# Two moves in a hand-ordered graph kernel: where one unit's selection matrices are made, and where a pair's overflow is taken

## The chip, the cores and the metric

The kernel runs on one core of a Trainium2 chip. A core has five engines that run side by side, each with its own queue of instructions: TensorE (PE, matrix products), VectorE (DVE), ScalarE (ACT), GpSimd (POOL) and SyncE (SP, which issues DMAs). [...] The metric is the device time of one execution in microseconds (us).

## The reference

One layer of message passing on a graph of 6250 nodes and 200000 edges, 128 features:

```python
h = jnp.maximum(_layernorm(x), 0.0)
xw = h @ W_in                                                  # one row per node
W_ij = (softplus(f_ij @ W_f1 + b_f1) - LOG2) @ W_f2 + b_f2     # one row per edge
x_ij = xw[dst] * (W_ij * edge_weight1)
out = jax.ops.segment_sum(x_ij, src, num_segments=6250)        # edges summed by src
y = x + (softplus(out @ W_o1 + b_o1) - LOG2) @ W_o2 + b_o2
```

`dst` is sorted, `src` is not: the sum over `src` is what the kernel spends most of its order on.

## The kernel before

The edges are taken in 391 quads of 512. A quad goes through a pipeline of some five stages, written as one Python loop over items `i`, fully unrolled: item `i` runs the first stage of quad `i`, the second of quad `i - 1`, and so on. Each engine gets its instructions in exactly the order in which the loop writes them; nothing reorders them, and the framework only adds the semaphores and, where a buffer is used again, the wait for its last reader.

Inside an item there are named points, in this order: `L`, `D0`, (`s1_oh`), `D1`, (`s2_pe_x`, `s2_pe_w`, `s1_pe`: matmuls L494, L497, L505, L313), (`s1_exp`, `s1_ln`: L318, L323), `A0`, `A1`, (`s2_copy`: four copies L510 into `xc`), `DM`, (`s2_m`: product L520 of `W` and `xc`), `PE1`, `PE2`, `A2`, `D2`, (scatters), `S`. `at(i, point, fn, ...)` hangs a step on a point of an item; steps on the same point run in the order in which they were hung there.

Edges are summed by `src` in two ways.

- *Plain and listed quads* (223 of 391) are written to DRAM by scatters that add: four DMAs with an index per row for each quad, issued by POOL (`scatter`, L582), whose source tile `s` has four buffers.
- *Grouped quads* (168 of them, `mpq`) are added on the chip. Their distances are 2, 2, 2 and 3 items, so the order repeats every 9 items. Call an item's place its distance from the first grouped quad of its round of four: grouped quads stand at places 0, 2, 4 and 6, and place 0 follows place 8. For a grouped quad `q`, item `q + 1` writes its product into a tile `pt` (L520) and makes four permutation matrices `pm` on DVE (`perm_oh`, L662); item `q + 2` splits the product into three bf16 parts (`part_rem`, two L676 on DVE, and the small `part_ext`, L682 on ACT); from item `q + 3` on PE permutes the edges into slots (`permute`, four times four matmuls L687) and ACT copies the result (`perm_out`, L693, into `mst`). `pm` and `pt` have two buffers each.

Slots can overflow. For each pair of grouped quads (the two at places 0 and 2, or at 4 and 6) `over_pe` collects the overflow rows of both quads in one product (eight matmuls L700 into `po`), and `over_out` copies it out on ACT (L707). Five items later the overflow is summed and scattered too (`over_idx` L714, `over_dg`, `over_row`, `over_eq`, `over_sum` L738 to L740, `over_copy` L745, `over_ji` L750, `over_int` L754).

Every 8 grouped quads (two rounds of four, 18 items) there are four *units*. A unit, at place 2 or at place 6 of a round (`UOFF = (2, 6)`), multiplies the permuted tiles of 8 quads with 8 selection matrices (`unit_pe`, 96 small matmuls L780 into four PSUM buffers `un`) and DVE adds the result to the sum on the chip in the item behind (`unit_evac`, four L791). The selection matrices `so` are made on DVE by `unit_oh` (one L765 each), in two halves of four.

PSUM tiles with the tag "B" share four buffers: `pq`, `po`, `un`, `orow`, `osum`, and the tiles of some rarer steps, among them the preparation of node rows (`prep_tp` L218, `prep_mm` L231) and the counting for the lists (`l_count` L378). A unit needs all four at once.

```python
def over_pe(q):
    qs = mpq[mpi[q] // 2 * 2:mpi[q] + 1]
    t = ps.tile([P, 512], F32, tag="B", name="po", bufs=4)
    for c in range(4):
        for h, p in enumerate(qs):
            nc.tensor.matmul(t[h * OVC:(h + 1) * OVC, :PW], mp[p]["pm"][:, c, GRP * CAP:],
                             high(mp[p]["pt"][:, c:c + 1, :PW])[:, 0], start=(c == 0), stop=(c == 3))
    mp[q]["po"] = t, len(qs) * OVC
```

After the loop a short tail adds the four DRAM sums and runs the last two layers.

Of the kernel before, what the change touches and what calls it, by code (L numbers as in the profile page):

```python
# [27 lines left out]
MP0 = 8  # L28
MPGAPS = (2, 2, 2, 3)
# [4 lines left out]
UOFF = (2, 6)  # L34
# [20 lines left out]
def tile_gnn(ctx: ExitStack, tc: tile.TileContext, x, fB, cT, srcT, srcr, dstr, win_, wf1, wf2, bias, bo1c, wo1,  # L55
# [25 lines left out]
    mpq = sorted_quads(NQ)  # L81
    mpi = {q: n for n, q in enumerate(mpq)}
# [752 lines left out]
    with tc.manual_schedule():  # L835
# [112 lines left out]
        def at(i, point, fn, *a):  # L948
            hooks.setdefault((i, point), []).append((fn, a))
# [136 lines left out]
        if spread:  # L1086
            k = clear(mid + 9, busy, 2)
# [3 lines left out]
            k = clear(NQ - 1, busy, 2)  # L1091
# [21 lines left out]
        for r in range(-(-len(mpq) // RKQ)):  # L1113
            i = mpq[RKQ * r]
            at(i - 5, "D2", rank_group, r)
            k = clear(i - 4, units)
            at(k, "PE2", rank_count, r)
            at(k + 1, "D0", rank_own, r)
            k = clear(k + 1, units)
# [5 lines left out]
        for w in range((LE - LB) // SW):  # L1125
# [25 lines left out]
            k = clear(i + 1, units)  # L1151
# [10 lines left out]
        for q in mpq:  # L1162
            at(q + 1, "D2", perm_oh, q)
            at(q + 2, "D2", part_rem, q, 1)
            at(q + 2, "D2", part_rem, q, 2)
            at(q + 2, "A2", part_ext, q)
            if q + 4 in units:
                for s in range(4):
                    at(q + 3, "PE2", permute, q, s)
                for s in range(4):  # L1170
                    at(q + 3, "PE2", perm_out, q, s)
            else:
                for s in range(4):
                    at(q + 3 + s // 2, "PE2", permute, q, s)
                    at(q + 4 + s // 2, "A0", perm_out, q, s)
            if mpi[q] % 2 or q == mpq[-1]:
                at(q + 3, "PE1", over_pe, q)
                at(q + 3, "PE1", over_out, q)
                at(q + 5, "DM", over_idx, q)
                at(q + 6, "A0", over_dg, q)  # L1180
                k = clear(q + 6, units)
                at(k, "PE2", over_row, q)
                at(k + 1, "D0", over_eq, q)
                k = clear(q + 8, units)
                at(k, "PE2", over_sum, q)
                at(k + 1, "A0", over_copy, q)
                at(k + 1, "DM", over_ji, q)
                at(k + 1, "A2", over_int, q)
                at(k + 2, "S", over_scatter, q)
        last = mpq[-1]  # L1190
        for r in range(len(mpq) // RND):
            for s, k in enumerate(unit_slots(mpq, r)):
                at(k - 2, "D2", unit_oh, r, s, 0)
                at(k - 1, "D2", unit_oh, r, s, 1)
                at(k, "PE2", unit_pe, r, s)
                at(k + 1, "D1", unit_evac, r, s)
# [79 lines left out]
    with tc.For_i(0, trips, 1) as ci:  # L1276
# [55 lines left out]
        s = wk.tile([P, P], F32, bufs=1, tag="dg", name="fs")  # L1332
# [112 lines left out]
def sorted_quads(nq):  # L1445
    qs, q = [], MP0
    while q < nq - MPEND:
        qs.append(q)
        q += MPGAPS[(len(qs) - 1) % len(MPGAPS)]
    return qs if len(qs) % RND <= EXTRA else qs[:len(qs) // RND * RND]  # L1450
# [7 lines left out]
def unit_slots(qs, r):  # L1458
    if r == len(qs) // RND - 1:
        return [qs[-1] + 6 + 2 * s for s in range(4)]  # L1460
    per, end = sum(MPGAPS), qs[RND * r + RND - 1] + 5
    return [i for i in range(end, end + 4 * per) if (i - MP0) % per in UOFF][:4]
# [12 lines left out]
def clear(i, busy, n=1):  # L1475
    while any(i + k in busy for k in range(n)):
        i += 1
    return i
# [113 lines left out]
```

## Time and profile before

| what | value |
|---|---|
| timed runs (3) | 2068.21, 2069.33, 2073.08 us; median 2069.33 us |
| the profiled execution | 2067.92 us, its span 2066.1 us |
| mean granted TensorE clock | 0.961 |
| busy: PE, DVE, ACT, POOL | 1815.0, 1658.7, 1468.1, 1648.0 us |
| scatters on POOL (L582): listed, plain, overflow | 768, 123, 96 |

All rows of the profile are of that one execution. "Busy" is the time in which an engine executes something; waiting and issuing do not count. A line `L582` is a line of the kernel's file. In the timelines a row gives the start and the length in us, the engine, the line, the operation, what it writes and reads, how many instructions the row joins, and in brackets how long the engine had been idle and what ended that. Matmuls are pipelined and their ends are modelled, so neighbouring rows of PE can overlap a little.

### The profile page before, as it was taken

To read this page: it belongs to the slowest core of one execution; us is meant where nothing else is said; L and a number is where in the kernel's file an instruction comes from. 1 tells how busy PE (TensorE), PEld (TensorE's weight loads), DVE (VectorE), ACT (ScalarE), POOL (GpSimd) and SP (SyncE) were. 2 spreads that over 40 slices of the span, in tenths; PEclk is the share of its full clock that TensorE was granted. 3 is DMA by queue.
4 is the path that set the end of the run, shared out by engine and by line. 5 is a ranking of instruction groups with operands and counts; after the bars stand their busy time and mean duration, and the time that the engine had idled before them with its cause. 6 is when DMAs were issued, how large, how long until landed. Compare 5 with 4: busy or idle time off the path is not lost. (4 is left out here: it accounts for less than half of the span.)

```text
span 2066.1 us, 54971 instructions
## 1 busy us (share of the span) xinstructions
PE 1815.0 (88%) x19121; PEld 1190.5 (58%) x19121; DVE 1658.7 (80%) x4448; ACT 1468.1 (71%) x3999; POOL 1648.0 (80%) x1040
## 2 busy tenths in 40 slices
PE   3589899989988999999899899899998999999956
PEld 2455556556655666555566566565665666566734
DVE  3678788888987888888888888879889788787745
ACT  3368676877776788777778777777777777788714
POOL 3578888888888788887788888888888888888774
PEclk9679999999999999999999999999999999999978
DMA  6887666667666666666667676676766666666649
GB/s 242 226 212 153 120 119 118 130 110 136 126 124 116 117 139 123 125 123 122 118 123 132 118 131 116 115 132 107 136 120 119 117 119 118 101 121 131 131 46 243
DMA packets 381177, 272.39 MB, mean 132 GB/s; under 512 B 97727, under 2 KB 341354, under 8 KB 380898
## 3 DMA queue, kind: packets, MB, share of 16 engines
q0 software_dynamic: 143728, 71.30, 34.6%
q1 hardware_dynamic: 236882, 197.50, 33.0%
q8 instruction: 151, 2.47, 0.5%
q14 instruction: 128, 1.05, 0.2%
q10 hardware_dynamic: 288, 0.07, 0.0%
HBM read 154.45 MB, written 114.24 MB: 130 GB/s over the span
## 5 line engine op out<-in xcount | busy, mean ns | idle before, releaser
L582 POOL DMA_INDIRECT acc<-s,lji x768 | 1254.4, 1633 | 255.9 <-issue 191.3
L687 PE MATMUL pq<-pt,pm 128*128 128x387 bf16 x2688 | 535.7, 343 | 29.8 <-ACT pt L682 13.5
L510 ACT ACTIVATE xc<-xg,cb 128x128 f32<-128x128 f32 x1564 | 448.2, 377 | 89.9 <-PE xg L497 85.3
L505 PE MATMUL W<-w,a 128*128 128x128 f32 x3128 | 465.1, 293 | 0.0
L505 PEld LDWEIGHTS W<-w,a 128*128 128x128 f32 x3128 | 389.5, 196 | 42.2 <-issue 3.1
L780 PE MATMUL un<-so,mst 32*128 32x392 bf16 x8064 | 376.6, 329 | 19.8 <-DVE lbad L411 4.6
L687 PEld LDWEIGHTS <-pm 128*128 128x128 bf16 x2688 | 259.7, 100 | 217.0 <-issue 40.8
L693 ACT CAST mst<-pq 128x387 bf16<-128x387 f32 x672 | 302.3, 481 | 112.8 <-PE pq L687 110.8
L780 PEld LDWEIGHTS <-mst 32*128 32x128 bf16 x8064 | 230.9, 94 | 158.7 <-issue 59.2
L323 ACT ACTIVATE a<-a,con 128x512 f32<-128x512 f32 x391 | 282.3, 722 | 12.7
L582 POOL DMA_INDIRECT acc<-s,ji x123 | 197.4, 1605 | 78.3 <-issue 28.3
L318 ACT ACTIVATE a<-z 128x512 f32<-128x512 f32 x391 | 238.5, 610 | 24.6 <-PE z L313 14.5
L676 DVE TENSOR_TENSOR pt<-pt 128x512 f32<-128x512 f32 x336 | 231.7, 690 | 5.8
L662 DVE TENSOR_SCALAR pm<-iot,pos 128x576 bf16<-128x576 f16 x672 | 220.8, 390 | 0.0
L520 DVE TENSOR_TENSOR s<-W,xc 128x512 f32<-128x512 f32 x192 | 131.9, 687 | 81.0 <-ACT xc L510 61.1
L765 DVE TENSOR_SCALAR so<-iot,mst 128x392 bf16<-128x392 f16 x672 | 191.9, 345 | 5.7 <-PE un L780 5.6
L791 DVE TENSOR_TENSOR accT<-un,accT 128x392 f32<-128x392 f32 x320 | 158.5, 557 | 44.7 <-PE un L780 44.2
L582 POOL DMA_INDIRECT acc<-os,oji x96 | 154.6, 1610 | 29.4 <-issue 19.5
L497 PE MATMUL xg<-wn,oh 63*128 63x128 bf16 x1564 | 157.4, 222 | 17.5 <-ACT xc L510 10.0
L520 DVE TENSOR_TENSOR pt<-W,xc 128x512 f32<-128x512 f32 x168 | 115.4, 687 | 70.4 <-ACT xc L510 58.6
L313 PE MATMUL z<-ft,ws 123*128 123x512 bf16 x391 | 151.7, 388 | 15.3 <-DMA ft<-fsd 15.0
L494 PE MATMUL W<-b2rep,onesb 64*128 64x512 bf16 x391 | 154.0, 394 | 0.0
(209 smaller groups left out, 1975.7 us busy)
## 6 DMA issues: line engine op xcount, KB each, us to landing
rb<-reld SPq DMA_DIRECT2D x391, 64.0 KB
fsd<-f SPq DMA_DIRECT2D x49, 480.0 KB
ft<-fsd SPq DMA_DIRECT2D x195, 120.0 KB
sb<-src SPq DMA_DIRECT2D x169, 128.0 KB
fb<-in_fB_dram SPq DMA_DIRECT2D x49, 320.0 KB
ft<-fsd SPq DMA_DIRECT2D x195, 80.0 KB
wn<-tab SPq DMA_DIRECT2D x782, 15.8 KB
acc<-s,lji POOLq DMA_INDIRECT x768
```

Source lines behind the costliest of these rows:

```text
L318: nc.scalar.activation(a, st[q]["z"], AF.Exp)
L323: nc.scalar.activation(a, a, AF.Ln, bias=half, scale=0.5)
L505: nc.tensor.matmul(W[:, c, :], st[q]["a"][:, c * P:(c + 1) * P], w2, start=False, stop=(c == 3))
L510: nc.scalar.mul(xc[:, c, :], st[q]["xg"][:, c, :], late["c", q // CQ][:, 4 * (q % CQ) + c:4 * (q % CQ) + c + 1])
L520: nc.vector.tensor_tensor(m[:, :, :P], st[q]["W"], st[q]["xc"], op=ALU.mult)
L582: nc.gpsimd.indirect_dma_start(out=accs[k][:rows, :], out_offset=bass.IndirectOffsetOnAxis(ap=ji, axis=0), in_=s, in_offset=None, compute_ ...
L662: nc.vector.tensor_scalar(pm[:, c], iot[:, :SLOTS], rk[r]["pos"][:, 4 * j + c:4 * j + c + 1], None, op0=ALU.is_equal)
L676: nc.vector.tensor_tensor(pt[:, :, k * P:(k + 1) * P], a, high(a), op=ALU.subtract)
L687: nc.tensor.matmul(t[:, :PW], mp[q]["pm"][:, c, s * P:(s + 1) * P], high(mp[q]["pt"][:, c:c + 1, :PW])[:, 0], start=(c == 0), stop=(c == 3))
L693: nc.scalar.copy(mp[q]["ms", s][:, :PW], mp[q].pop(("q", s))[:, :PW])
L765: nc.vector.tensor_scalar(so, iotw[:, :GN], w[:, 3 * P // 2:3 * P // 2 + 1], None, op0=ALU.is_equal)
L780: nc.tensor.matmul(ts[g][:, :GN], mp[q]["ms", s][v, k * P:(k + 1) * P], mp[q]["oh"][v], start=(q == qs[0] and k == 0), stop=(q == qs[-1] a ...
```

## The change

Two points of the order move; no instruction is added, removed or altered.

- `over_pe` and `over_out` of a pair are hung on the item behind the next grouped quad instead of on item `q + 3` (`q` is the pair's second quad). For a pair whose second quad stands at place 2 that is the same item, place 5. For one whose second quad stands at place 6 it is one item later: place 1 instead of place 0.
- For a unit at place 6 (all but the very last units) the first half of the selection matrices is made in item `k - 1` instead of `k - 2`, so both halves, eight L765, stand one behind the other at place 5. Units at place 2 keep their halves in two items.

```diff
             if mpi[q] % 2 or q == mpq[-1]:
-                at(q + 3, "PE1", over_pe, q)
-                at(q + 3, "PE1", over_out, q)
+                k = mpq[mpi[q] + 1] + 1 if mpi[q] + 1 < len(mpq) else q + 3
+                at(k, "PE1", over_pe, q)
+                at(k, "PE1", over_out, q)
                 at(q + 5, "DM", over_idx, q)
...
             for s, k in enumerate(unit_slots(mpq, r)):
-                at(k - 2, "D2", unit_oh, r, s, 0)
+                at(k - (1 if (k - MP0) % sum(MPGAPS) == UOFF[1] and k < last else 2), "D2", unit_oh, r, s, 0)
                 at(k - 1, "D2", unit_oh, r, s, 1)
                 at(k, "PE2", unit_pe, r, s)
```

In the order of each engine this shows as follows. On PE the eight L700 of place 0 stand behind L313 of place 1, ahead of `over_sum`. On ACT L707 stands behind the four L510 of place 1 instead of those of place 0. On DVE four L765 leave their place behind L676 at place 4 and stand ahead of the other four behind L662 at place 5; L520 at place 1 gets a wait for L700 in place of one for L505. POOL and SP keep their order.

## The prediction

> **What bounds the kernel now.** I read the page first, then the busy time by stretches, then what POOL waited for, and last the timelines of PE, DVE and ACT around the items that the diff touches. The page's first part names PE as the busiest engine:
>
> ```profile
> PE 1815.0 (88%) x19121; PEld 1190.5 (58%) x19121; DVE 1658.7 (80%) x4448; ACT 1468.1 (71%) x3999; POOL 1648.0 (80%) x1040
> ```
>
> PE has 88%, POOL 80%. That order misleads, because a scatter on POOL (L582) is never followed by the next one at once. What POOL waited for between 364 and 1210 us (columns: engine and line, releaser, us in total, times, longest):
>
> ```profile
> POOL acc L582 <- issue: 106.1, 348, 0.3
> POOL acc L582 <- DVE s L520: 15.1, 12, 2.9
> POOL acc L582 <- DVE bn L186: 8.1, 6, 3.7
> ```
>
> The first row is a fixed pause: 106.1 / 348 = 0.305 us before a scatter, with nothing to wait for. Only the other two rows are waits for data, and both are the product of item `q` (`s2_m`, L520) coming too late. So a scatter holds POOL for its own time and 0.305 us. With that price the busy time by stretches (each row: the stretch, its length, then busy us and count of PE, PEld, DVE, ACT, POOL) reads differently:
>
> ```profile
> 364.00:660.00 296.00, 270.23 (x2908) 174.27 (x2907) 251.18 (x699) 223.35 (x616) 249.62 (x153) 0.98 0.68 123
> 660.00:1210.00 550.00, 506.82 (x5523) 329.89 (x5520) 474.56 (x1317) 412.55 (x1134) 448.29 (x276) 0.98 0.67 124
> 1210.00:1765.00 555.00, 515.46 (x5677) 333.53 (x5674) 468.84 (x1230) 418.36 (x1130) 467.76 (x287) 0.99 0.66 120
> 1765.00:1900.00 135.00, 130.20 (x1354) 87.22 (x1353) 107.18 (x270) 112.07 (x311) 113.34 (x72) 0.98 0.67 116
> 1900.00:2007.00 107.00, 88.85 (x1038) 62.58 (x1035) 67.38 (x176) 54.38 (x159) 86.04 (x56) 0.93 0.58 97
> ```
>
> POOL's time with the pauses: 249.62 + 153 x 0.305 = 296.3 of 296; 448.29 + 276 x 0.305 = 532.5 of 550; 467.76 + 287 x 0.305 = 555.3 of 555; 113.34 + 72 x 0.305 = 135.3 of 135; 86.04 + 56 x 0.305 = 103.1 of 107. In three of the five stretches the scatters stand end to end, and what PE, DVE and ACT save there shortens nothing: it only lengthens the queue in front of POOL. POOL ran dry for 17.5 us between 660 and 1210 and for 3.9 us at the end. The granted clock is 0.98 in the first of these, so the clock is no term here. Ahead of 364 us I count nothing, because the start-up sets the scatters there.
>
> So the change can bring at most 17.5 + 3.9 = 21.4 us, and it brings what it takes off the chain of PE, DVE and ACT from about 364 to 1210 us (before that POOL's queue is full; from there to 660 it drains, so a lead won there is kept) and in the last 240 us.
>
> **Part 1: the overflow product.** Places count the items from a round of four grouped quads, 0 to 8. `over_pe` (eight matmuls, L700) and its copy `over_out` (L707) move from place 0 to place 1, for one pair in two; the pair at place 5 stays, and so does every other instruction of the pair. Work is neither added nor removed, so the question is what waits. PE at a place 0 (start, us, engine, line, what; in brackets the idle time and who ended it):
>
> ```profile
> 951.95 0.38 PE L313 MATMUL z<-ft,ws 123*128 123x512 bf16 x1
> 952.26 0.36 PE L700 MATMUL po<-pt,pm 128*64 128x387 bf16 x1
> 953.69 0.86 PE L700 MATMUL po<-pt,pm 128*64 128x387 bf16 x7 [1.07 <-DVE pt L676]
> 954.48 0.71 PE L231 MATMUL xps<-win_sb,h 128*128 128x128 f32 x4
> 955.03 0.54 PE L378 MATMUL lcnt<-wgtb,eql 128*128 128x1 bf16 x16
> 955.43 0.86 PE L687 MATMUL pq<-pt,pm 128*128 128x387 bf16 x4
> ```
>
> The first of the eight runs, the other seven wait for the remainders (`part_rem`, L676) of the pair's second quad. The permutations behind them (L687) read the same remainders, so the wait does not vanish: it passes to L687. What changes is that the work between them, which does not need the remainders (L231 and L378, 955.43 - 954.48 = 0.95 us), now runs inside the wait. L313 ends at 952.33, L231 and L378 at 953.28, and L687 starts at 953.69 instead of 955.43. Of those 1.74 us, 0.79 (953.69 to 954.48) are `over_pe` and come back in the next item; 0.95 us are won. Where a place 0 has no wait, or nothing between, nothing is won.
>
> Between 364 and 1210 us there are 19 places 0. Seven have both a wait and work between. The first and the last of them, by the same reading (the pair's matmuls are over where L231 starts):
>
> ```profile
> 414.22 0.71 PE L231 MATMUL xps<-win_sb,h 128*128 128x128 f32 x4
> 414.76 0.54 PE L378 MATMUL lcnt<-wgtb,eql 128*128 128x1 bf16 x16
> 415.17 0.33 PE L687 MATMUL pq<-pt,pm 128*128 128x387 bf16 x1
> ```
>
> ```profile
> 1130.00 0.49 PE L231 MATMUL xps<-win_sb,h 128*128 128x128 f32 x2
> 1130.33 0.54 PE L378 MATMUL lcnt<-wgtb,eql 128*128 128x1 bf16 x16
> 1130.73 0.33 PE L687 MATMUL pq<-pt,pm 128*128 128x387 bf16 x1
> ```
>
> That is 0.95 and 0.73 us. The seven, each the smaller of wait and work, are 0.95, 0.48, 0.48, 0.83, 0.15, 0.95 and 0.73: 4.6 us. The last 240 us hold three more places 0; the estimate for them is one such gain, 0.9 us (bounds 0 and the 3.9 us that POOL was dry).
>
> The move puts a new wait on DVE and puts `over_out` behind `xc` on ACT. ACT, DVE and PE at places 1 and 2 of the same round:
>
> ```profile
> 957.40 1.15 ACT L510 ACTIVATE xc<-xg,cb 128x128 f32<-128x128 f32 x4
> 958.41 0.43 ACT L248 CAST x<-rm 128x256 bf16<-128x256 f32 x1
> 958.71 0.64 ACT L318 ACTIVATE a<-z 128x512 f32<-128x512 f32 x1
> 959.37 0.72 ACT L323 ACTIVATE a<-a,con 128x512 f32<-128x512 f32 x1
> 960.00 0.25 ACT L745 COPY os<-osum 128x132 f32<-128x132 f32 x1
> 960.15 0.87 ACT L693 CAST mst<-pq 128x387 bf16<-128x387 f32 x2
> ```
>
> ```profile
> 958.58 0.69 DVE L520 TENSOR_TENSOR pt<-W,xc 128x512 f32<-128x512 f32 x1 [1.54 <-ACT xc L510]
> ```
>
> ```profile
> 961.45 0.38 PE L313 MATMUL z<-ft,ws 123*128 123x512 bf16 x1
> 961.76 0.35 PE L780 MATMUL un<-so,mst 32*128 32x392 bf16 x4
> ```
>
> DVE: `part` has two buffers, so the grouped product at place 1 (the L520 above) overwrites the tile that `over_pe` still reads, and must wait until `over_pe` is through. Behind it on DVE stand `perm_oh` (L662), four selection matrices (L765) and the next `oh`. Today it waits anyway, 1.54 us for `xc`. After the change item 1 begins 1.74 us earlier, `xc` with it, and `over_pe` is done about 0.9 us before 958.58 (1.74 less its own 0.79). So the new wait takes the place of the old one and ends earlier. That lead on DVE pays only where DVE, not PE, is the last to arrive at the unit's evacuation: bounds 0 and 2.4 us over the 19 rounds, and I take 1, nearer to 0, since the evacuation mostly waits for the unit itself.
>
> ACT: the unit at place 2 (L780) needs all four PSUM buffers, and the last to be freed is the second L693, at 961.02, 0.74 us before 961.76. `over_out` is a copy of the same shape as one of the two L693 (0.87 / 2 = 0.44 us) and now stands between L510 and L248. With `over_pe` done at about 957.7, `over_out` ends at about 958.2 and the five behind it, 2.61 us from 958.41 to 961.02, at 960.8; the unit, 0.95 earlier, wants to start at 960.8. The slack is used up to nothing. Bounds: 0, and the whole 0.44 at each of 19 + 5 units; I take 0.5 us in all, nearest to the row.
>
> **Part 2: the selection matrices at place 6.** Four L765 leave place 4 and stand in front of the other four at place 5, behind L520 and `perm_oh`. Nothing else moves with them. DVE at places 4 to 6 of another round:
>
> ```profile
> 1021.99 1.41 DVE L676 TENSOR_TENSOR pt<-pt 128x512 f32<-128x512 f32 x2
> 1023.32 1.05 DVE L765 TENSOR_SCALAR so<-iot,mst 128x392 bf16<-128x392 f16 x4
> 1024.29 0.68 DVE L520 TENSOR_TENSOR pt<-W,xc 128x512 f32<-128x512 f32 x1
> 1024.89 0.81 DVE L284 TENSOR_TENSOR f<-fr,f 128x640 bf16<-128x640 f32 x1
> 1025.62 1.25 DVE L662 TENSOR_SCALAR pm<-iot,pos 128x576 bf16<-128x576 f16 x4
> 1026.79 1.27 DVE L765 TENSOR_SCALAR so<-iot,mst 128x392 bf16<-128x392 f16 x4
> ```
>
> ```profile
> 1029.39 0.34 PE L780 MATMUL un<-so,mst 32*128 32x392 bf16 x3
> ```
>
> ```profile
> 1029.78 0.22 DVE L750 SCALAR_TENSOR_TENSOR ojd<-os,con,ojd 128x1 f32<-128x1 f32 x1 [1.31 <-ACT os L745]
> 1030.82 0.69 DVE L520 TENSOR_TENSOR s<-W,xc 128x512 f32<-128x512 f32 x1 [0.82 <-ACT xc L510]
> ```
>
> The remainders are made before the four L765, so `over_pe` at place 5 is not helped. L520 waits for `over_pe` and would not start earlier than 1024.29 here; DVE would stand idle for the 1 us that the four now fill, and everything behind would come 1.05 us later: L765 ends at 1029.1 instead of 1028.0. The unit starts at 1029.39 and takes its matrices one after the other, and L750 waited 1.31 us for ACT: 1.05 fits under both. If that cover is gone (rounds where DVE is late at place 6), the cost is bounded by the same 1.05 us; but in those rounds DVE reaches L520 after `over_pe` is done, so nothing idles and the order alone changes. I take 0 for all, bounds -1 and +3 us.
>
> A scatter beside such a run, from the same stretch:
>
> ```profile
> 1026.24 1.54 POOL L582 DMA_INDIRECT acc<-s,lji  x1 [0.31 <-issue]
> ```
>
> It ran with `perm_oh` and L765 all along and took 1.54 us, less than the mean (448.29 / 276 = 1.62). [...]
>
> **The sum.** 4.6 + 0.9 + 1.0 - 0.5 + 0 = 6.0 us less. The profiled execution took 2067.92 us (span 2066.1), below the three timed runs (median 2069.33); it would take 2061.9, and the median 2063.3. A measurement of this kernel can tell about 0.3% (6.2 us) from no change, so the forecast lies right beside that bound.
>
> **Rivals.** *Wider gain* (12%): the lead on DVE and the freer ACT at place 0 also carry through places 3 to 8, and POOL hardly runs dry: 12 to 20 us, about 2054. For it: both L520 rows wait for ACT. Against: the remainders that PE waits for at place 5 do not move. *No gain* (11%): the filler at place 0 waits for its own inputs, or the lead is lost at the next wait for L676: 2069. *ACT holds the unit at place 2* (15%, slower): the second L693 ends later than the unit could start. The place is the unit behind `over_out`; there are 24 of them in the two stretches that count. From 5.5 / 24 = 0.23 us late each it eats the gain, from (5.5 + 6.2) / 24 = 0.49 it makes the kernel slower by over 0.3%; at 0.7 (`over_out` and its wait for `over_pe`) it costs 24 x 0.7 - 5.5 = 11 us: 2080. For it: the slack of 0.74 is the only one. Against: item 1 starts earlier on ACT by the wait that `over_out` leaves behind at place 0. [...]
>
> **How the numbers follow.** The forecast has 60%; its own range is 2059 to 2068 (4.6 less some 3 us for ACT or for Part 2 leaves 1.6; 4.6 with 1.9 at the end, 2.4 on DVE and 1 from Part 2 makes 10), and 26 of the 60 lie below 2063.1. Faster: 26 + 12 = 38%. Same: 34 + 11 = 45%. Slower: 15 + 2 = 17%. The range, 2053 to 2074, leaves out a third of the wider gain and most of the slower cases.
>
> **What would show it.** Right: at place 0 the wait for L676 stands before L687, with L231 and L378 ahead of it; L520 at place 1 waits for `over_pe`; POOL's wait for L520 between 660 and 1210 falls from 23 us to about 18 while its busy time stays. Wrong: L780 at place 2 waits for ACT's L693; scatters longer than before; POOL's waits for L520 as large as now or in new stretches.

## The result, and the profile after

| | before | with the change |
|---|---|---|
| median of 9 runs | 2069.33 us (2064.84 to 2075.11) | 2056.89 us (2052.48 to 2061.75) |
| the profiled execution | 2067.92 us, span 2066.1 | 2059.12 us, span 2057.4 |

The ratio is 0.9934 with a 95% interval of 0.9916 to 0.9953: the change makes the kernel faster by 0.66%, by the medians 12.4 us. The prediction's sum was 6.0 us less, 2063.3 us. The direction was right and the size about half of what came. The two profiled executions show 8.8 us of it.

The first part of the page, with the change:

```profile
PE 1808.0 (88%) x19121; PEld 1183.3 (58%) x19121; DVE 1657.7 (81%) x4448; ACT 1472.2 (72%) x3999; POOL 1642.0 (80%) x1040
```

What POOL waited for between 364 and 1210 us, and its busy time in the stretch in which it ran dry (POOL's pair of numbers is the fifth):

```profile
POOL acc L582 <- issue: 102.8, 337, 0.3
...
POOL acc L582 <- DVE s L520: 6.9, 7, 2.5
POOL acc L582 <- DVE bn L186: 6.4, 3, 3.2
```

```profile
660.00:1210.00 550.00, 509.24 (x5547) 329.96 (x5547) 476.58 (x1322) 417.14 (x1144) 454.64 (x278) 0.98 0.68 124
```

The waits for `s` fell from 15.1 + 8.1 to 6.9 + 6.4 us, and with the pause POOL's time is 454.64 + 278 x 0.305 = 539.4 of 550 instead of 532.5: 10.6 us dry instead of 17.5. That is 6.9 us of the 8.8.

PE at the same place 0 as in the prediction, and the two items behind it:

```profile
945.07 0.38 PE L313 MATMUL z<-ft,ws 123*128 123x512 bf16 x1
945.29 0.61 PE L231 MATMUL xps<-win_sb,h 128*128 128x128 f32 x4
945.73 0.54 PE L378 MATMUL lcnt<-wgtb,eql 128*128 128x1 bf16 x16
946.81 1.57 PE L687 MATMUL pq<-pt,pm 128*128 128x387 bf16 x8 [0.54 <-DVE pt L676]
...
949.95 0.89 PE L700 MATMUL po<-pt,pm 128*64 128x387 bf16 x8
...
954.08 3.16 PE L780 MATMUL un<-so,mst 32*128 32x392 bf16 x72
```

L231 and L378 stand inside the wait, of which 0.54 us is left. L700 runs an item later without a wait, and from L313 to the unit it takes 954.08 - 945.07 = 9.01 us instead of 961.76 - 951.95 = 9.81. DVE and ACT at place 1:

```profile
950.94 0.69 DVE L520 TENSOR_TENSOR pt<-W,xc 128x512 f32<-128x512 f32 x1 [1.67 <-PE po L700]
```

```profile
950.91 0.48 ACT L707 CAST mo<-po 128x387 bf16<-128x387 f32 x1 [0.96 <-PE po L700]
...
953.00 0.87 ACT L693 CAST mst<-pq 128x387 bf16<-128x387 f32 x2
```

L520 waits for `over_pe` now, but starts 950.94 - 945.07 = 5.87 us after L313 where it took 6.63. The second L693 ends at 953.87, 0.21 us ahead of the unit: the slack of 0.74 us shrank and held.

The place 6 of the prediction's second set of rows (DVE, then the unit on PE):

```profile
1014.23 1.41 DVE L676 TENSOR_TENSOR pt<-pt 128x512 f32<-128x512 f32 x2
1016.77 0.69 DVE L520 TENSOR_TENSOR pt<-W,xc 128x512 f32<-128x512 f32 x1 [1.14 <-PE po L700]
...
1019.23 2.43 DVE L765 TENSOR_SCALAR so<-iot,mst 128x392 bf16<-128x392 f16 x8
...
1023.37 0.22 DVE L750 SCALAR_TENSOR_TENSOR ojd<-os,con,ojd 128x1 f32<-128x1 f32 x1 [1.31 <-ACT os L745]
```

```profile
1022.98 1.25 PE L780 MATMUL un<-so,mst 32*128 32x392 bf16 x19
```

Where four L765 stood before L520, DVE idles 1.14 us; the eight end at 1021.66, the unit starts at 1022.98, and L750 waits for ACT by the same 1.31 us as before.

### The profile page after: what moved, and what is told of

Same layout as the page of the kernel before. It is cut to its first block, busy times and chain, and to the rows that moved or that the text cites. A ratio compares the mean times of both kernels' runs of the same rounds, so it can differ in the third digit from the quotient of the medians.

```text
span 2057.4 us, 54972 instructions
## 1 busy us (share of the span) xinstructions
PE 1808.0 (88%) x19121; PEld 1183.3 (58%) x19121; DVE 1657.7 (81%) x4448; ACT 1472.2 (72%) x3999; POOL 1642.0 (80%) x1040
## 5 line engine op out<-in xcount | busy, mean ns | idle before, releaser
L510 ACT ACTIVATE xc<-xg,cb 128x128 f32<-128x128 f32 x1564 | 449.5, 378 | 86.2 <-PE xg L497 83.7
L505 PE MATMUL W<-w,a 128*128 128x128 f32 x3128 | 465.6, 293 | 0.0
L505 PEld LDWEIGHTS W<-w,a 128*128 128x128 f32 x3128 | 389.9, 196 | 42.3 <-issue 3.3
L780 PE MATMUL un<-so,mst 32*128 32x392 bf16 x8064 | 371.0, 325 | 18.9 <-ACT s L540 4.5
L693 ACT CAST mst<-pq 128x387 bf16<-128x387 f32 x672 | 303.5, 482 | 115.6 <-PE pq L687 112.7
L780 PEld LDWEIGHTS <-mst 32*128 32x128 bf16 x8064 | 225.0, 93 | 158.1 <-issue 52.6
L676 DVE TENSOR_TENSOR pt<-pt 128x512 f32<-128x512 f32 x336 | 231.9, 690 | 5.8
L662 DVE TENSOR_SCALAR pm<-iot,pos 128x576 bf16<-128x576 f16 x672 | 222.0, 392 | 0.0
L520 DVE TENSOR_TENSOR s<-W,xc 128x512 f32<-128x512 f32 x192 | 132.0, 687 | 84.1 <-ACT xc L510 71.4
L765 DVE TENSOR_SCALAR so<-iot,mst 128x392 bf16<-128x392 f16 x672 | 183.5, 337 | 8.0 <-PE un L780 7.9
L520 DVE TENSOR_TENSOR pt<-W,xc 128x512 f32<-128x512 f32 x168 | 115.6, 688 | 88.5 <-PE po L700 52.9
L313 PE MATMUL z<-ft,ws 123*128 123x512 bf16 x391 | 152.2, 390 | 16.0 <-DVE iotl L940 9.3
L494 PE MATMUL W<-b2rep,onesb 64*128 64x512 bf16 x391 | 154.5, 395 | 0.0
```

Of the source, the lines that this page charges most:

```text
L505: nc.tensor.matmul(W[:, c, :], st[q]["a"][:, c * P:(c + 1) * P], w2, start=False, stop=(c == 3))
L510: nc.scalar.mul(xc[:, c, :], st[q]["xg"][:, c, :], late["c", q // CQ][:, 4 * (q % CQ) + c:4 * (q % CQ) + c + 1])
L520: nc.vector.tensor_tensor(m[:, :, :P], st[q]["W"], st[q]["xc"], op=ALU.mult)
L662: nc.vector.tensor_scalar(pm[:, c], iot[:, :SLOTS], rk[r]["pos"][:, 4 * j + c:4 * j + c + 1], None, op0=ALU.is_equal)
L676: nc.vector.tensor_tensor(pt[:, :, k * P:(k + 1) * P], a, high(a), op=ALU.subtract)
L693: nc.scalar.copy(mp[q]["ms", s][:, :PW], mp[q].pop(("q", s))[:, :PW])
```

## The experiments

All of them ran against the kernel before on the same chip. The chips differ (the kernel before had medians from 2069.3 to 2078.1 us), so ratios are compared. The code excerpts show the lines that matter.

| kernel | median us | ratio | 95% interval |
|---|---|---|---|
| the change | 2056.89 | 0.9934 | 0.9916 to 0.9953 |
| before, again | 2071.87 | 1.0008 | 0.9989 to 1.0027 |
| Part 1 alone | 2057.06 | 0.9937 | 0.9916 to 0.9958 |
| Part 2 alone | 2071.39 | 1.0004 | 0.9990 to 1.0018 |
| product behind the filler | 2071.22 | 1.0000 | 0.9983 to 1.0018 |
| copy an item later | 2072.96 | 0.9989 | 0.9973 to 1.0004 |
| both of these | 2069.29 | 0.9961 | 0.9940 to 0.9982 |
| change in items 50 to 229 only | 2066.67 | 0.9959 | 0.9941 to 0.9978 |
| change in items 230 to 349 only | 2077.20 | 0.9996 | 0.9979 to 1.0012 |
| before, tiles read earlier | 2070.05 | 0.9959 | 0.9939 to 0.9980 |
| change, tiles read earlier | 2062.32 | 0.9913 | 0.9885 to 0.9942 |
| change, remainders first | 2064.54 | 0.9928 | 0.9902 to 0.9954 |
| change, both of these | 2064.95 | 0.9931 | 0.9907 to 0.9956 |

A second table is worked out from the traces. For the 18 rounds between 364 and 1210 us it sums the length of the items (from the first L494 of one to that of the next) by their place, and beside that stand POOL's waits for L520 and L186 in that stretch, in us:

| kernel | places 0, 1 | place 2 | places 3 to 8 | POOL's waits |
|---|---|---|---|---|
| before | 153.6 | 114.9 | 534.2 | 23.2 |
| before, again | 153.7 | 113.0 | 536.4 | 25.9 |
| Part 2 alone | 152.3 | 114.8 | 535.3 | 21.0 |
| the change | 149.1 | 109.7 | 533.2 | 13.3 |
| Part 1 alone | 148.3 | 109.5 | 532.0 | 16.5 |
| product behind the filler | 150.6 | 119.8 | 533.8 | 24.8 |
| copy an item later | 154.5 | 115.4 | 535.5 | 25.1 |
| both of these | 149.7 | 118.0 | 531.8 | 15.7 |
| before, tiles read earlier | 153.2 | 106.0 | 540.5 | 17.8 |
| change, tiles read earlier | 149.3 | 104.4 | 542.1 | 16.3 |
| change, remainders first | 147.3 | 111.4 | 537.2 | 4.7 |
| change, both of these | 148.0 | 106.7 | 537.3 | 2.3 |
| change in items 50 to 229 only | 150.2 | 111.9 | 536.1 | 19.5 |
| change in items 230 to 349 only | 152.1 | 113.0 | 540.6 | 28.2 |

The last two rows serve as a further trace of each side, since these 18 rounds are items 62 to 223: the first has the change in all of them, the second in none. Each row is one execution, and the rows of one side differ by up to 2.4 us at place 2 and by 6 to 7 us in POOL's waits.

**The kernel before, again.**

> The kernel before, once more, unchanged: it gives a second profile and says how far two executions of one kernel lie apart. Time 2069 +- 3 us. If the difference of 12.4 us between the medians, of which the two profiled executions show 8.8, is in the waits of POOL, then between 364 and 1210 us POOL's waits for L520 and for L186 sum to 21 to 25 us again (23.2 in the first profile, 13.3 with the change), and the scatter before which 300 others stand starts at 661 +- 2 us. If the rest of the difference is scatter time that varies from execution to execution, the sum of the scatters' own time differs by 3 to 6 us from 1606.4.

Its waits were 25.9 us, a little above the range, the scatter before which 300 others stand started at 665.8 us, 3 us outside its range, and POOL was busy for 1643.9 us where the first profile has 1648.0. The change and Part 1 alone have 1642.0 and 1641.3. So 8.5 us of the gain stand in POOL's waits (23.4, the mean of the first three rows, against 14.9, the mean of the next two), and some 4 us in the scatters' own time. With two profiles on the one side that last part is not shown; the change in the middle items alone has 1648.3.

**Part 1 alone, Part 2 alone.** The two hunks of the diff, one at a time.

> Part 1 alone: the overflow product and its copy one item later, the selection matrices as before. Theory A (the filler at place 0 runs inside the wait for L676, Part 2 is worth nothing): 2055 to 2060 us, all of the gain, POOL's waits for L520 and L186 between 364 and 1210 us at 12 to 15 us. Rival B (both parts share the gain, since eight L765 in a row leave DVE free for the remainders at place 4): 2062 to 2064 us. Rival C (Part 2 is the whole gain): 2069 us.

> Part 2 alone: the first half of the selection matrices at place 5, the overflow product as before. Theory A: 2069 +- 3 us; L520 at place 5 waits for L700 in most rounds (12 us in all between 364 and 1210 us instead of 3.6) and nothing behind it is later, as L791 at place 6 waits 2 us in all as before. Rival B: 2062 to 2064. Rival C: 2057. A cost that Part 1 covers would show as 2072 to 2078.

Part 1 is the whole gain, Part 2 is worth nothing that can be measured: theory A had the shares right, and rivals B and C fall. POOL's waits, 16.5 us, lie a little above the 12 to 15 expected. What inside Part 1 pays is the question of the next three runs. What DVE waited for in Part 2 alone, and in the kernel before:

```profile
DVE pt L520 <- PE po L700: 11.7, 10, 2.0
```

```profile
DVE pt L520 <- PE po L700: 3.6, 4, 1.0
```

The idle 8 us on DVE are there, and no cost of them can be seen: the ratio is 1.0004.

**The product behind the filler.**

```diff
-    at(q + 3, "PE1", over_pe, q); at(q + 3, "PE1", over_out, q)
+    at(q + 3, "PE2", over_pe, q); at(q + 3, "PE2", over_out, q)   # second pair only, ahead of permute
```

> The kernel before, with one step moved inside place 0: the overflow product of the second pair stands behind the preparation and counting matmuls (L231, L378) and still ahead of the permutations (L687); it stays in its item, and so does its copy. Theory A (what is won is that this filler runs inside the wait for L676): the same gain as Part 1 at the seven places 0 of the prediction, and no new wait at place 1: 2055 to 2062 us. Rival D (the gain comes from the copy and the product leaving place 0, that is from ACT and DVE at place 0): no gain, 2067 to 2071 us.

This missed: no gain. PE did win at place 0 (153.2, the mean of the first three rows, to 150.6), and place 2 took it all back (114.2 to 119.8). ACT at place 0 of the round shown, before:

```profile
954.59 0.48 ACT L707 CAST mo<-po 128x387 bf16<-128x387 f32 x1 [2.31 <-PE po L700]
```

ACT, then the unit at place 2, with the product behind the filler:

```profile
954.04 0.48 ACT L707 CAST mo<-po 128x387 bf16<-128x387 f32 x1 [2.29 <-PE po L700]
...
959.46 0.87 ACT L693 CAST mst<-pq 128x387 bf16<-128x387 f32 x2
```

```profile
960.29 4.22 PE L780 MATMUL un<-so,mst 32*128 32x392 bf16 x96
```

ACT stands for 2.29 us at the copy (2.31 before), so little behind it is earlier. PE arrives sooner and meets the second L693, which ends at 960.33, 0.04 us after the unit's start. It ends after the unit's start in all 18 rounds of this trace (by 0.04 to 0.99 us), in four of the kernel before and in one with the change. In rounds without a wait the filler only delays the product, and ACT with it. Some 0.8 us of the 5.6 at place 2 is not ACT's: the units of items 73 and 217 stood still a little longer, and both ran at half clock (see below). A cover on PE is not enough, then: here ACT holds the unit, since its copy still waits at place 0.

**The copy later, alone and with the product behind the filler.**

```diff
-    at(q + 3, "PE1", over_out, q)
+    at(q + 4, "PE1", over_out, q)   # second pair only
```

> The kernel before with the copy of the overflow product alone one item later (place 1, behind L510); the product itself stays at place 0 ahead of L231 and L378. Together with the run before (product behind the filler, copy at place 0) this makes a table of two edits. Theory E (two chains: PE wins 0.95 us at place 0 only if ACT, which stands behind the copy's wait at place 0, is released as well): ACT gains alone, PE does not; units at place 2 start as before, and the time is 2065 to 2070 us. Theory D (ACT alone is the gain): 2055 to 2060. Theory A (PE alone is the gain): 2069 to 2071.

> Both edits of the table: the product at place 0 behind L231 and L378, the copy at place 1. The product does not leave its item. Theory E: all of the gain of Part 1, 2055 to 2060 us; places 0 to 2 of the 18 rounds between 364 and 1210 us take 258 us as in Part 1 alone (267 before, 270 with the product alone behind the filler), and ACT's last copy is done before the unit begins. If the product has to leave place 0 altogether (its eight matmuls in the wait for L676 are what PE wins): 2065 to 2070.

Alone the copy brings at most a little, with the product 0.4%, where the two single edits give 0 and 0.1%. That is the sign that theory E expects, but the intervals are too wide to show that the two edits need each other, and it is not all of the gain. The 258 us at places 0 to 2 were missed (267.7), and the trace says why. PE at place 0 of the same round, both edits:

```profile
955.68 0.86 PE L687 MATMUL pq<-pt,pm 128*128 128x387 bf16 x4 [0.57 <-ACT mst L693]
```

With its copy at place 1, `po` holds one of the four "B" buffers through place 0. In the items 71, 107, 179 and 215, where L231 and L378 need one each, the second permutation waits 0.57 us for a buffer; no other kernel of the two tables up to here has that wait there. So neither half of the step does what the whole does: the product and its copy have to leave place 0 together. The gain that this trace has at places 3 to 8 (531.8) is within what single executions differ by.

**Where it is made.** `50 <= q < 230` or `230 <= q < 350` as a further condition of the first hunk, and the same for `k` in the second.

> The whole change, but only for pairs and units of items 50 to 229, that is from about 330 to 1200 us; elsewhere as before. If scatters that stand end to end make the rest worthless (POOL is the bound from 1210 to 1900 us), nearly all of the gain is here: 2056 to 2061 us. If each round gains wherever it stands (19 of 41 rounds): 2063 to 2065.

> The whole change, but only for pairs and units of items 230 to 349, that is from about 1200 to 1765 us. If POOL is the bound there: 2068 to 2072 us, as before, and the scatter before which 930 others stand starts as far behind the one with 600 before it as in the kernel before (636 us). If each round gains wherever it stands (13 of 41 rounds): 2065 to 2066.

The late rounds are worth nothing that can be measured, the middle ones 0.41%. The scatter with 930 before it starts 639 us behind the one with 600 before it, no sooner than the 636 of the kernel before. POOL is the bound from 1210 us on, as the prediction had it. The middle rounds give less than the whole (0.66%), with intervals that overlap; what the first 50 and the last 40 items add is not settled.

**Two tiles read earlier.** The table of places has a second term that the prediction did not: place 2 lost 4.6 us (114.2 to 109.6), most of it in the items 73 and 217. There a unit stands still. PE in item 217 of the kernel before, again:

```profile
1138.34 0.34 PE L780 MATMUL un<-so,mst 32*128 32x392 bf16 x3
1140.94 5.81 PE L780 MATMUL un<-so,mst 32*128 32x392 bf16 x93 [2.25 <-DVE lbad L411]
```

and with the change:

```profile
1131.07 0.34 PE L780 MATMUL un<-so,mst 32*128 32x392 bf16 x3
1132.78 4.13 PE L780 MATMUL un<-so,mst 32*128 32x392 bf16 x93 [1.37 <-DVE loh L409]
```

After three matmuls the unit needs its fourth PSUM buffer, and that is still held by the tile of `l_before`, whose readers L407 and L409 stand on DVE at place 2, behind L520, `perm_oh` and the selection matrices of place 1. With the change L520 stands earlier, and so do they. L520 and L409 on DVE, the kernel before again, then with the change:

```profile
1135.77 0.69 DVE L520 TENSOR_TENSOR pt<-W,xc 128x512 f32<-128x512 f32 x1 [2.19 <-ACT xc L510]
...
1140.45 0.44 DVE L409 TENSOR_SCALAR loh<-iotl,lpre 128x135 bf16<-128x135 f16 x1
```

```profile
1127.91 0.69 DVE L520 TENSOR_TENSOR pt<-W,xc 128x512 f32<-128x512 f32 x1 [1.13 <-PE lpre L400]
...
1132.47 0.26 DVE L409 TENSOR_SCALAR loh<-iotl,lpre 128x135 bf16<-128x135 f16 x1
```

L520 starts 2.57 us before the unit in the one and 3.16 in the other, L409 2.11 and 1.40 us behind the unit's start. The second thing in PE's rows is the length of the other 93 matmuls, 5.81 against 4.13 us. The granted clock (the third number from the right) over the first of them:

```profile
1140.90:1142.60 1.70, 1.66 (x33) 1.12 (x36) 1.53 (x9) 0.00 (x0) 1.40 (x2) 0.80 0.43 36
1142.60:1144.30 1.70, 1.70 (x28) 1.07 (x24) 1.70 (x6) 1.50 (x4) 1.39 (x2) 0.50 0.39 34
1144.30:1146.70 2.40, 2.40 (x47) 1.42 (x39) 1.45 (x4) 0.58 (x3) 2.10 (x2) 0.78 0.70 211
```

Behind the stall PE is granted half its clock for 3.41 us, and the unit loses 1.68 us more. To test this, the readers were moved ahead of `perm_oh`:

```diff
-        nc.vector.tensor_scalar(oh[:, :P + LCAP], iotl, pre, None, op0=ALU.is_equal)
+        nc.vector.tensor_scalar(oh[:, :P + LCAP], iotl, pre, None, op0=ALU.is_equal); yield   # l_index in two steps
...
-            at(i + 1, "D0", l_index, w)
+            g = l_index(w)
+            at(*((i, "D2") if i + 1 in units else (i + 1, "D0")), next, g, None)
+            at(i + 1, "D0", next, g, None)
...
-            at(i + 1, "D0", l_take, w)
+            at(*((i, "D2") if i + 1 in units else (i + 1, "D0")), l_take, w)
```

> The kernel before, with two readers of PSUM tiles taken earlier: where the item behind holds a unit, the first two instructions of l_index (L407, L409, which read the tile of l_before) and the one of l_take (L444, which reads the tile of l_place) stand on DVE at place 1 ahead of perm_oh instead of at place 2 behind the eight of perm_oh and the selection matrices. Nothing else moves; that is three units between 364 and 1210 us (items 73, 163, 217). Theory F (the gain at place 2 that the prediction lacked comes from these units, which stand still for 1.6 to 2.5 us for their fourth PSUM buffer and after that run at half clock in some executions, 1.7 us each): the stalls fall below 0.5 us, no unit at items 73, 163 and 217 at half clock, places 0 to 2 of the 18 rounds 6 to 9 us below 267 us, time ratio 0.996 to 0.998. Rival (the stall passes to the selection matrices, which are 0.5 us later, or to POOL, which is not dry any earlier): ratio 0.999 to 1.001.

> The same two earlier reads on top of the whole change. Theory F: the stalls that are left there, 1.8, 1.6 and 1.4 us, go, and with them the chance of half clock: 4 to 6 us more than the change alone, ratio to the kernel before 0.990 to 0.992 (0.9934 without). Rival: 0.993 to 0.995.

Item 217 of the kernel before with the earlier reads:

```profile
1133.03 4.30 PE L780 MATMUL un<-so,mst 32*128 32x392 bf16 x96
```

All 96 run without a pause. Place 2 fell from 114.2 to 106.0 us: a few small instructions on DVE, moved past eight others, are worth 0.4% by themselves. On top of the change the ratio is 0.9913, the lowest of all kernels here, but its interval overlaps that of the change alone, so what the two reads add to the change is not settled. Part of what the units win comes back behind them: places 3 to 8 took 540.5 and 542.1 us, about 2 us more in each of the rounds of items 71 and 215.

**The remainders first.** PE's largest wait for data with the change is for L676 at place 5.

```diff
-            at(q + 2, "D2", part_rem, q, 1)      # and q, 2
+            at(q + 2, "DM", part_rem, q, 1)
```

> The whole change, and part_rem (two L676) in item q + 2 ahead of the product L520 of that item instead of behind it. PE waits 18 us for L676 at place 5 in 14 of 18 rounds between 364 and 1210 us. If that wait is what is late next: L676 is done 0.7 us earlier or more where L520 waits for xc, the wait falls by a half, and the ratio is 0.988 to 0.991. Rival (L520 at place 4 and 8, a source of scatters, is 0.7 to 1.4 us later, and POOL is dry there): 0.993 to 0.998.

> The whole change with the earlier reads and with part_rem ahead of L520. If both are worth what their theories say: ratio 0.984 to 0.989. If the remainders ahead of L520 cost, this is slower than the change with the earlier reads alone.

PE's wait for L676 between 364 and 1210 us, with the change alone:

```profile
PE po L700 <- DVE pt L676: 18.0, 14, 2.7
```

PE's wait, POOL's waits and the page's first part, change with the remainders first:

```profile
PE po L700 <- DVE pt L676: 0.5, 1, 0.5
```

```profile
POOL acc L582 <- DVE bn L186: 3.8, 2, 2.0
...
POOL acc L582 <- DVE s L520: 0.9, 1, 0.9
```

```profile
PE 1820.2 (88%) x19121; PEld 1191.3 (58%) x19121; DVE 1651.8 (80%) x4448; ACT 1463.5 (71%) x3999; POOL 1656.4 (80%) x1040
```

The wait of 18 us is gone and POOL waits 4.7 us instead of 13.3, but POOL is busy for 1656.4 us instead of 1642.0: the scatters themselves take longer, and the time stays (0.9928 where theory and rival said 0.988 to 0.991 and 0.993 to 0.998). The kernel with both edits has 1656.4 as well; all the other profiles lie between 1641.3 and 1648.7. Neither theory foresaw that. Both edits were expected at 0.984 to 0.989 and gave 0.9931; whether the remainders cost something on top of the earlier reads is not settled.

PE keeps little of what it wins, either. Place 5 took 122.1 us instead of 136.8, but place 6, where the next unit stands, 125.9 instead of 112.6. What these units waited for between 364 and 1210 us, with the change and with the remainders first:

```profile
PE un L780 <- DVE pr L627: 1.2, 3, 0.4
```

```profile
PE un L780 <- DVE pr L627: 7.8, 5, 1.9
```

It is the same picture as in the items 73 and 217: a PSUM tile that DVE reads (L627, a step of the ranks) holds the unit that now comes earlier, and three of these units run at half clock afterwards.

## Why the prediction was right or wrong

**What bounds the kernel.** Right. The same edit is worth 0.41% in the middle items and 0.04%, within its interval nothing, in those from 1200 to 1765 us, and POOL's waits for L520 and L186 fell where they were expected to: between 660 and 1210 us from 22.3 us to 12.6, where "about 18" was said.

**Part 1 on PE at place 0: 4.6 us.** The mechanism was right, and the agreement in size is partly luck: places 0 and 1 together went from 153.2 to 148.7 us, 4.5 less (3.7 with the two further traces). In the six of the seven listed rounds that no half-clock window touched in either profile, places 0 and 1 became 3.3 us shorter where 4.1 were listed. The seventh, at item 98, became 0.92 longer, with such a window; in Part 1 alone it became 0.40 shorter, with 0.48 listed. About 1.1 us of the 4.5 come from the other eleven rounds, some 0.1 us each, where nothing was said to be won.

**DVE: +1.0, ACT: -0.5.** Here the step failed. DVE's lead at place 1 was sized well (0.76 us, "about 0.9" was said), but it was weighed only at the evacuation behind the unit, with bounds of 0 and 2.4. Its main effect is ahead of it: in the items 73 and 217 the unit waits for a PSUM tile that DVE reads behind L520. By the traces the 4.6 us at place 2 are 1.2 from shorter stalls (2.28 and 2.25 us on average to 1.81 and 1.50), 2.8 from half-clock windows (five in three traces of kernels without Part 1, none in the two with it, up to 1.68 us each) and 0.6 from the rounds of the items 80, 143, 152 and 170. How much of the 2.8 is chance is open: the trace of the change in the middle items has one such window at item 73, and with it and its counterpart the windows make about 2 us. ACT cost nothing: the second L693 ended before the unit's start in 17 of the 18 rounds, where it had done so in 14; that is most of the 0.6. The rival in which ACT holds the unit did not come with the change. It came with the product behind the filler, where the copy stayed at place 0.

**"The clock is no term here."** Wrong. A mean of 0.98 over 550 us hides windows of half clock (0.50 granted for 3.41 us or a multiple of it) that stand in a few items, and some of these follow the stalls that the change shortens.

**The end: +0.9.** The profiles have 1.8 us there (the scatter with 900 before it starts 7.0 us earlier, the last one 8.8), too little to tell from chance: Part 1 alone against the kernel before, again, has 2.0 us the other way.

**Part 2: 0.** Right, with the mechanism as described: DVE idles at place 5 (its waits for L700 are 11.7 us in Part 2 alone where they were 3.6), and nothing behind it is later (the ratio is 1.0004).

**The rivals and the chances.** The result, 2056.89 us, lies inside the whole range but below the forecast's own 2059 to 2068, at the edge of the *wider gain* (12 to 20 us). That rival's mechanism did not come: places 3 to 8 took 533.2 and 532.0 us against 534.2 to 540.6 in the four traces that leave these rounds without any of Part 1, no more than single executions differ by, and the gain stands at places 0 to 2. The 2 of the 15 + 2 for slower stood for scatters that the units at place 6 hold up, and no run shows that: Part 2 alone has 1.0004 (0.9990 to 1.0018), and with the change the 47 scatters between 364 and 1210 us that ran beside L765 for 1 us or more took 1.62 us on average, the 346 beside none of it 1.63. Faster by over 0.3% had 0.38, and within 0.3% had 0.45. The forecast stood beside that bound, and the term left out carried the result across it.

## What to carry to other kernels

When an engine's step is moved off a wait, ask of every engine that shares the item whether it is released too: the cover on PE alone paid nothing, the copy moved alone nothing that can be measured, and product and copy moved together 0.6%. For each PSUM tile that a large consumer needs, look for the last reader and what stands ahead of that reader on its engine; here one to two small DVE instructions behind eight unrelated ones cost each of three units a stall (2.38, 1.58 and 2.25 us in the first profile of the kernel before). Read the granted clock over a few microseconds behind each long stall, not as a mean. When a wait is removed, look at once for the next tile that the engine, now earlier, will meet.

## What the runs showed of the hardware

- A stall on PE often cost more than its length. Of 13 units that stood still for 2.0 to 2.5 us (items 73, 163 and 217 in all fourteen traces), 9 ran at half clock (0.50 granted) afterwards; of 19 that stood for 1.3 to 1.9 us, 3; of 10 that hardly stood (0.23 us at most), none. With the remainders first, units at place 6 stall as well: of the eight in the items 113, 131, 149 and 185 of those two traces that stood for 1.5 to 1.95 us, five ran at half clock. Each such unit took 1.5 to 1.7 us longer, and the windows are 3.41 us long or a multiple. In each trace all windows between 364 and 1900 us start on one grid of 3.413 us (to within 1 ns), which lies differently in each execution. Sorted by the cells of that grid, the fourteen traces show when it comes: of 133 cells at full clock in which PE idled for 1.8 us or more in sum, 125 were followed by half clock, of 257 with 1.2 to 1.8 us, 47, and of over 4000 with less, 5 (in the first profile of the kernel before and the one with the change, between 364 and 1900 us: 17 of 17, 7 of 36 and none of 815). So, by these counts, a stall of much the same length cost up to 1.7 us more or nothing, mostly by how it lay in the grid: in the first profile of the kernel before the unit of item 73 stood for 2.38 us, 2.09 us of idle time fell into one cell, and half clock followed; the unit of item 217 stood for 2.25 us, which fell into two cells as 1.53 and 0.73, and ran on at full clock.
- The median scatter takes 1.54 us, some take longer, and the longer ones tend to stand beside certain instructions of DVE. Two scatters of the kernel with the change, and what DVE ran beside the first:

```profile
943.84 2.40 POOL L582 DMA_INDIRECT acc<-os,oji  x1 [0.30 <-ACT h L224]
...
1012.24 1.54 POOL L582 DMA_INDIRECT acc<-os,oji  x1 [0.30 <-ACT a L323]
```

```profile
943.61 1.21 DVE L369 TENSOR_TENSOR eql<-sb,srcT_sb 128x1024 bf16<-128x1024 int16 x1
...
945.34 1.41 DVE L676 TENSOR_TENSOR pt<-pt 128x512 f32<-128x512 f32 x2
```

Of the 987 scatters with the change, those that overlap L676 alone are on average 0.12 us longer than 1.54 (240 of them), those that overlap L369 alone 0.17 us (104), those that overlap both 0.41 us (36), and those that overlap neither 0.03 us (607). With the remainders first it is 0.15 us (195), 0.22 (105), 0.58 (30) and 0.04 (657). So none of the 14 us by which the scatters grew there stands beside L676 alone; about half stands beside L369, half beside neither, and the cause is open. No run took L676 or L369 away, so that they make these scatters longer is not shown. Beside the selection matrices nothing of the kind stands: between 364 and 1210 us the scatters that ran beside L765 for 1 us or more took 1.60 us on average before (50 of them) and 1.62 with the change (47), those beside none of it 1.63 in both (336 and 346).
